# Order of the weighted values and their sums in time attention, and of the first feed-forward products behind band attention

## The chip, the cores and the metric

The kernel runs on one core of a Trainium2 chip. The metric is the device time of one execution in microseconds (us); lower is better. All data is 32-bit floating point. TensorE (PE in the profile) does the matrix products, VectorE (DVE) and GpSimd (POOL) do elementwise work, ScalarE (ACT) evaluates functions, SyncE (SP) issues the transfers.

## The reference, cut to what matters

The input x has 2 batches, 256 times, 128 bands and 128 channels. Three blocks follow one another, each with a layer norm in front and a residual: attention over time (4 heads of 32 channels, causal), attention over the bands (4 heads, a query sees the keys within 16 bands), and a feed-forward of 512 hidden channels with gelu.

```python
def _mha(x, wi, bi, wo, bo, h, mask):
    c = x.shape[-1]; dh = c // h
    q, k, v = jnp.split(x @ wi.T + bi, 3, axis=-1)          # then split into heads
    scores = jnp.einsum('...hqd,...hkd->...hqk', q, k) * (1.0 / np.sqrt(dh)) + mask
    attn = jax.nn.softmax(scores, axis=-1)
    o = jnp.einsum('...hqk,...hkd->...hqd', attn, v)
    o = o.swapaxes(-2, -3).reshape(x.shape)
    return o @ wo.T + bo

xt = _ln(x, ln_t_w, ln_t_b).transpose(0, 2, 1, 3)
x = x + _mha(xt, t_wi, t_bi, t_wo, t_bo, 4, cm).transpose(0, 2, 1, 3)
xf = _ln(x, ln_f_w, ln_f_b)
x = x + _mha(xf, f_wi, f_bi, f_wo, f_bo, 4, bm)
xn = _ln(x, ln_n_w, ln_n_b)
h = jax.nn.gelu(xn @ w1.T + b1, approximate=False)
x = x + (h @ w2.T + b2)
```

## The kernel before

The work is cut into groups of 512 positions: 128 groups of time attention (`OverTime`), then 16 runs, each of 8 groups of band attention (`OverBands`) and the 8 groups of feed-forward (`FeedForward`) on the same data. The groups pass through a software pipeline: iteration n does the scores of group n, the weighted values of group n-1, the output product of group n-2 and the projections of group n+1. Every engine takes its instructions in program order. A product is written to one of eight banks of PSUM, which are handed out in turn.

A product with 128x128 weights can be made as one matmul or as four with 32 weight columns each (128*32 in the profile), which run side by side. `product` does the latter:

```python
def product(path, out, weights, x):
    for c in range(P // D):                       # P = 128, D = 32
        path.tensor.matmul(out[rows_of(c)], weights[:, rows_of(c)], x, start=True, stop=True)
```

It serves `queries_keys` (banks qp, kp), `values` (vp) and `output` (yp) of both attentions. The scores (sp) use 32 rows of the array for each head. The feed-forward uses full matmuls: four products hp for the hidden channels, and sixteen small ones into zp.

In time attention a group has two sequences s of 256 times. The weights p of one sequence and head are three blocks of 128 keys by 128 queries, and a fourth block holds the sum of blocks 1 and 2, so that one matmul with ones makes the softmax denominators (rp) of both query halves. GpSimd adds that block for s = 0 (in `first_mask`), VectorE for s = 1 (`last_sum`, the last step of an iteration):

```python
    def add(self, engine, s):
        engine.tensor_tensor(self.block(s, 3), self.block(s, 1), self.block(s, 2), ALU.add)

    def weigh(self):                                          # OverTime
        path = self.path
        p, v, W = self.p, self.v, self.W
        rp = path.bank([P, 2, 2 * P], "rp")
        sums = p.rearrange("p s h (n q) -> p s h n q", q=P)[:, :, :, 0:4:3, :]
        for h in range(H):
            path.tensor.matmul(rp[rows_of(h), :, :], path.k.ones[:, 0:D], sums[:, :, h], start=True, stop=True)
        op = path.bank([P, 2, 2 * P], "op")
        for s in range(2):
            ...                                               # weighted values of sequence s into op
```

The denominators are inverted on ScalarE, as exp(-ln), and refined on VectorE while the values are divided (the profile calls the tile r0 "r"). The weights of the output product have a minus sign that undoes the sign of oT:

```python
    def invert(self):
        ...
        path.scalar.activation(ln, self.rp, AF.Ln)
        path.scalar.activation(self.r0, ln, AF.Exp, scale=-1.0)

    def divide(self):
        ...
        vector.tensor_tensor(by_rows(t), by_tile(self.rp), by_tile(self.r0), ALU.mult)
        vector.tensor_tensor(by_rows(u), by_tile(self.op), by_tile(self.r0), ALU.mult)
        vector.scalar_tensor_tensor(self.oT, t, 2.0, u, ALU.subtract, ALU.mult)
```

Band attention masks its weights pf outside the band: GpSimd with two selects for each of the first heads (`first_mask`), VectorE with one product for the last `by_vector` heads (`second_mask`); `by_vector` is 1, and 2 in the last group of a run. Its `weigh` makes rp, then op.

The feed-forward makes its four hp in two halves:

```python
    def first_half(self):
        self.hp = {}
        self.hT = ...
        self.hidden((0, 1))          # hp 0 and 1; first_function: their gelus
    def second_half(self):
        self.hidden((2, 3))          # hp 2 and 3; second_function: their gelus
```

The loop of the pipeline; `feeds[2]` says that group n is a feed-forward group, `bands[2]` that it is a band group, index 1 means group n-1; A is 8:

```python
        for n in range(-11, len(groups) + 2):
            feeds = [at(n - 2 + i, FeedForward) for i in range(5)]
            bands = [at(n - 2 + i, OverBands) for i in range(5)]
            do(n + 11, "load")
            do_at(n + 4, OverTime, "statistics")
            if bands[2] and feeds[1]:
                self.scalar.preload_act_table_set(EXP_SET)
            do(n, "first_half", "first_function", "first_mask")
            do_at(n + 2, Attention, "fetch")
            do_at(n + 1, FeedForward, "fetch")
            do_at(n + 2, FeedForward, "normalize", "turn")
            do_at(n + 3, Attention, "normalize", "turn")
            do_at(n + 3, FeedForward, "statistics", "root")
            do_at(n + 4, OverTime, "root")
            if bands[2]:
                do(n, "second_mask")
            do(n - 1, "weigh")
            if not feeds[1]:
                do(n - 1, "invert")
            if bands[2]:
                do(n - 2, "output", "finish")
            do(n - 1, "divide")
            do(n, "second_half", "second_function")
            if not bands[2]:
                do(n, "second_mask", "bias")
                do_at(n + A, OverBands, "bias", "statistics", "root")
            do(n + 1, "queries_keys", "take_query", "take_key")
            if not bands[2]:
                do(n - 2, "output", "finish")
            do(n + 1, "values", "take_values")
            do(n, "last_sum")
```

A group's normalized data xh is turned through memory: VectorE transposes it within 32x32 squares (z), it is written out (turned) and fetched back as xnT an iteration later.

Of the kernel before, what the change touches and what calls it, by code (L numbers as in the profile page):

```python
# [10 lines left out]
F32 = mybir.dt.float32  # L11
# [9 lines left out]
H = 4  # L21
# [414 lines left out]
class Group:  # L436
# [95 lines left out]
    def weigh(self):  # L532
        pass
# [4 lines left out]
    def divide(self):  # L538
        pass
# [8 lines left out]
class Attention(Group):  # L548
# [38 lines left out]
    def invert(self):  # L587
# [4 lines left out]
        self.r0 = path.work.tile([P, NT * P], F32, name="r0", bufs=2)  # L592
        path.scalar.activation(self.r0, ln, AF.Exp, scale=-1.0)

    def divide(self):

        path, vector = self.path, self.path.vector
        t = path.work.tile([P, NT * P], F32, name="t", bufs=2)
        vector.tensor_tensor(by_rows(t), by_tile(self.rp), by_tile(self.r0), ALU.mult)
        u = path.work.tile([P, NT * P], F32, name="u", bufs=2)  # L600
        vector.tensor_tensor(by_rows(u), by_tile(self.op), by_tile(self.r0), ALU.mult)
        self.oT = path.work.tile([P, NT * P], F32, name="oT", bufs=2)
        vector.scalar_tensor_tensor(self.oT, t, 2.0, u, ALU.subtract, ALU.mult)
# [16 lines left out]

def product(path, out, weights, x):

    for c in range(P // D):
        path.tensor.matmul(out[rows_of(c)], weights[:, rows_of(c)], x, start=True, stop=True)


class OverTime(Attention):
# [63 lines left out]
    def last_sum(self):  # L691
        self.add(self.path.vector, 1)

    def weigh(self):
        path = self.path
        p, v, W = self.p, self.v, self.W
        rp = path.bank([P, 2, 2 * P], "rp")
        sums = p.rearrange("p s h (n q) -> p s h n q", q=P)[:, :, :, 0:4:3, :]
        for h in range(H):
            path.tensor.matmul(rp[rows_of(h), :, :], path.k.ones[:, 0:D], sums[:, :, h], start=True, stop=True)  # L700
        op = path.bank([P, 2, 2 * P], "op")
        for s in range(2):
            for h in range(H):
                r = rows_of(h)
                path.tensor.matmul(op[r, s, :], v[:, 2 * s, r], p[:, s, h, 0 : 2 * P], start=True, stop=False)
            for h in range(H):
                r = rows_of(h)
                path.tensor.matmul(
                    op[r, s, P : 2 * P], v[:, 2 * s + 1, r], p[:, s, h, 2 * P : W], start=False, stop=True
                )  # L710
        self.op = op.rearrange("p s q -> p (s q)")
        self.rp = rp.rearrange("p s q -> p (s q)")

# [122 lines left out]
class BoundedPath:  # L836
# [38 lines left out]
    def groups(self, x, out):  # L875
# [29 lines left out]
        for b in range(B):  # L905
            for r0 in range(0, T, RUN):
                run = []
                for t0 in range(r0, r0 + RUN, GB):
                    held = {}


                    def load(g, t0=t0, b=b, held=held):
                        if g == 0:
                            self.quad(held, "x", 4)
                            self.quad(held, "x2", 2 * RUN // GB)
                        for i in range(2 * g, min(2 * g + 2, NT)):
                            nc.sync.dma_start(
                                held["x"][rows_of(i)].rearrange("q g t c -> q (g t) c"),
                                self.of_bands(k.x1[b], t0 + NT * i, NT),
                            )  # L920

                    def store(g, t0=t0, b=b, held=held):
                        for i in range(NT if g % 2 else 0):
                            nc.sync.dma_start(
                                self.of_bands(out[b], t0 + NT * i + g - 1, 2),
                                held["res"][rows_of(i), g - 1 : g + 1].rearrange("q g t c -> q (g t) c"),
                            )

                    def part(name, g, held=held):
                        if name == "res" and name not in held:  # L930
                            self.quad(held, "res", 2)
                        return held[name][:, g]

                    run += [(g, part, load, store) for g in range(NT)]
                for i, (g, part, load, _) in enumerate(run):
                    group = OverBands(self, partial(part, "x", g), partial(part, "x2", g), partial(load, g))
                    if i == len(run) - 1:
                        group.by_vector = 2
                    yield group
                for g, part, _, store in run:  # L940
                    yield FeedForward(self, partial(part, "x2", g), partial(part, "res", g), None, partial(store, g))

    def run(self, x, out):
        groups = list(self.groups(x, out))

        def do(n, *names):
            if 0 <= n < len(groups):
                for name in names:
                    getattr(groups[n], name)()

        def at(n, kind):
            return 0 <= n < len(groups) and isinstance(groups[n], kind)

        def do_at(n, kind, *names):
            if at(n, kind):
                do(n, *names)

        A = RUN // NT

        self.scalar.preload_act_table_set(EXP_SET)  # L960
        for n in range(-11, len(groups) + 2):
            feeds = [at(n - 2 + i, FeedForward) for i in range(5)]
            bands = [at(n - 2 + i, OverBands) for i in range(5)]
            do(n + 11, "load")
            do_at(n + 4, OverTime, "statistics")
            if bands[2] and feeds[1]:
                self.scalar.preload_act_table_set(EXP_SET)
            do(n, "first_half", "first_function", "first_mask")
            do_at(n + 2, Attention, "fetch")
            do_at(n + 1, FeedForward, "fetch")  # L970
            do_at(n + 2, FeedForward, "normalize", "turn")
# [3 lines that stand above are left out]
            if bands[2]:  # L975
                do(n, "second_mask")
            do(n - 1, "weigh")
            if not feeds[1]:
                do(n - 1, "invert")
            if bands[2]:  # L980
                do(n - 2, "output", "finish")
            do(n - 1, "divide")
            do(n, "second_half", "second_function")
            if not bands[2]:
                do(n, "second_mask", "bias")
                do_at(n + A, OverBands, "bias", "statistics", "root")
            do(n + 1, "queries_keys", "take_query", "take_key")
            if not bands[2]:
                do(n - 2, "output", "finish")
            do(n + 1, "values", "take_values")  # L990
            do(n, "last_sum")
# [69 lines left out]
```

## Time and profile before

| What | Value |
|---|---|
| time, median of 3 runs | 2832.48 us (2829.37 to 2876.43) |
| span of the profiled execution | 2826.2 us, 107020 instructions |
| TensorE clock granted | 0.998 of full speed |
| time attention, start of the first rp to that of the last | 54.23 to 1056.75 us, 128 groups |
| a run of 8 band groups and 8 feed-forward groups | about 110 us, 16 of them |
| transfers | 343.90 MB, mean 122 GB/s |

The profile calls a group of instructions by its engine and by the tiles it writes and reads, out<-in: sp, rp, op, qp, kp, vp, yp, hp and zp are the products named above, pt the weights of time attention, pf those of band attention, hT the gelus' output. A row of the timeline gives the start, the duration, the engine, the operation, the tiles, the shapes and how often, with the idle time before it in brackets. Nearly all instructions have one line number, that of a helper, so the tiles tell them apart. Matmuls are pipelined, so the durations of two successive stages overlap; how long a stage holds up the next is read from the distance between two starts. A full-precision product counts as two matmul instructions.

### The profile page before, as it was taken

To read this page: it belongs to the slowest core of one execution; us is meant where nothing else is said; L and a number is where in the kernel's file an instruction comes from. 1 tells how busy PE (TensorE), PEld (TensorE's weight loads), DVE (VectorE), ACT (ScalarE), POOL (GpSimd) and SP (SyncE) were. 2 spreads that over 40 slices of the span, in tenths; PEclk is the share of its full clock that TensorE was granted. 3 is DMA by queue.
4 is the path that set the end of the run, shared out by engine and by line. 5 is a ranking of instruction groups with operands and counts; after the bars stand their busy time and mean duration, and the time that the engine had idled before them with its cause. 6 is when DMAs were issued, how large, how long until landed. Compare 5 with 4: busy or idle time off the path is not lost.

```text
span 2826.2 us, 107020 instructions
## 1 busy us (share of the span) xinstructions
PE 2757.7 (98%) x44070; PEld 1858.9 (66%) x44070; DVE 2264.5 (80%) x6462; ACT 1865.2 (66%) x3408; POOL 2057.9 (73%) x2537
## 2 busy tenths in 40 slices
PE   5999999999999989999999999999999999999998
PEld 3666666666666656766766766666667667667666
DVE  5888888888888898788787787786887877877874
ACT  2777777777777767557557566566575575675664
POOL 3999999999999996676675676676666766656762
PEclk9999999999999999999999999999999999999999
DMA  5455545454554544534434434534435445344333
GB/s 122 126 148 133 140 129 146 131 140 130 147 140 129 135 126 123 144 105 106 128 106 120 129 102 122 131 94 130 115 101 141 106 107 130 102 121 114 87 95 84
DMA packets 471313, 343.90 MB, mean 122 GB/s; under 512 B 43296, under 2 KB 405152, under 8 KB 470816
## 3 DMA queue, kind: packets, MB, share of 16 engines
q1 hardware_dynamic: 469568, 335.92, 45.6%
q8 instruction: 349, 5.72, 0.8%
q14 instruction: 148, 1.21, 0.2%
q10 hardware_dynamic: 1248, 1.05, 0.1%
HBM read 169.03 MB, written 167.77 MB: 119 GB/s over the span
## 4 chain that ended last, share of the span: by engine, by line
PE 93%; DMA 2%; POOL 2%; DVE 2%; issue 0%; SPq 0%; ACT 0%; DVEq 0%; POOLq 0%
PE zp L831 16%; PE hp L831 16%; PE sp L831 13%; PE op L831 9%; PE rp L831 9%; PE qp L831 8%; PE yp L831 7%; PE vp L831 7%; PE kp L831 7%; DMA xnT<-turned 1%; DVE xh L831 1%; POOL pf L831 1%; POOL rstd L831 1%; DMA x<-in_x 1%; POOL pt L831 1%; DMA turned<-z 0%
## 5 line engine op out<-in xcount | busy, mean ns | idle before, releaser
L831 POOL TENSOR_SCALAR_AFFINE_SELECT pf<-pf 128x512 f32<-128x512 f32 x736 | 495.4, 688 | 273.1 <-ACT pf L831 248.0
L831 ACT ACTIVATE hT<-hp,b 128x512 f32<-128x512 f32 x512 | 345.2, 687 | 479.8 <-PE hp L831 470.3
L831 DVE TENSOR_SCALAR xh<-x,mv,rstd 128x128 f32<-128x128 f32 x1536 | 621.7, 465 | 15.4 <-POOL rstd L831 15.4
L831 PEld LDWEIGHTS zp<-w2T_sb,hT 128*128 128x128 f32 x4096 | 476.9, 192 | 56.1 <-issue 51.6
L831 ACT ACTIVATE pt<-sp 128x384 f32<-128x384 f32 x1024 | 419.6, 497 | 104.6 <-PE sp L831 104.6
L831 POOL TENSOR_TENSOR rstd<-rstd,mhalf 128x4 f32<-128x4 f32 x384 | 463.5, 1207 | 32.0
L831 PE MATMUL zp<-w2T_sb,hT 128*128 128x128 f32 x4096 | 480.4, 276 | 0.1
L831 PE MATMUL hp<-xnT,w1f 128*128 128x512 f32 x1024 | 474.8, 599 | 3.3 <-DMA xnT<-turned 3.0
L831 PE MATMUL sp<-qT,kT 32*128 32x128 f32 (+1 forms) x8192 | 398.3, 317 | 0.9 <-ACT kT L831 0.8
L831 POOL TENSOR_SCALAR_AFFINE_SELECT pt<-pt 128x512 f32<-128x512 f32 x512 | 315.3, 636 | 96.6 <-ACT pt L831 96.6
L831 PEld LDWEIGHTS sp<-qT,kT 32*128 32x128 f32 x8192 | 316.5, 186 | 85.8 <-issue 31.8
L831 DVE BATCH_NORM_STATS2 stats<-x 128x6 f32<-128x128 f32 x1536 | 326.8, 273 | 7.8 <-DMA x<-in_x 7.8
L831 POOL TENSOR_SCALAR rstd<-mv 128x4 f32<-128x4 f32 x384 | 94.9, 247 | 318.3 <-DVE mv L831 318.3
L831 ACT ACTIVATE pf<-sp 128x512 f32<-128x512 f32 x512 | 264.4, 603 | 62.5 <-PE sp L831 58.5
L831 PEld LDWEIGHTS hp<-xnT,w1f 128*128 128x128 f32 x1024 | 180.9, 190 | 176.9 <-issue 103.9
L831 PE MATMUL qp<-xnT,wf 128*32 128x512 f32 x2048 | 271.5, 602 | 26.1 <-DMA xnT<-turned 26.1
L831 PEld LDWEIGHTS yp<-wn,oT 128*32 128x32 f32 x8192 | 229.1, 110 | 99.6 <-issue 51.0
L831 DVE STREAM_TRANSPOSE z<-xh 128x512 f32<-128x512 f32 x384 | 273.2, 711 | 18.8 <-DMA turned<-z 5.6
L831 PEld LDWEIGHTS vp<-wf,xnT 128*32 128x32 f32 x8192 | 232.1, 110 | 78.2 <-issue 68.6
L831 DVE TENSOR_TENSOR pf<-pf,band 128x512 f32<-128x512 f32 x144 | 127.1, 892 | 188.8 <-ACT pf L831 181.3
L831 PE MATMUL yp<-wn,oT 128*32 128x128 f32 x8192 | 271.4, 273 | 0.0
L831 PE MATMUL vp<-wf,xnT 128*32 128x128 f32 x8192 | 270.6, 273 | 0.0
(87 smaller groups left out, 4029.4 us busy)
## 6 DMA issues: line engine op xcount, KB each, us to landing
turned<-z SPq DMA_DIRECT2D x1536, 64.0 KB, 2.0
xnT<-turned SPq DMA_DIRECT2D x384, 256.0 KB, 2.7
x<-in_x SPq DMA_DIRECT2D x128, 256.0 KB, 4.7
x<-res SPq DMA_DIRECT2D x256, 128.0 KB, 3.4
x<-x SPq DMA_DIRECT2D x128, 256.0 KB, 4.2
out<-res SPq DMA_DIRECT2D x256, 128.0 KB, 2.8
w1T_sb<-in_w1T ACTq DMA_DIRECT2D x1, 256.0 KB, 3.4
w2T_sb<-in_w2T ACTq DMA_DIRECT2D x1, 256.0 KB, 3.9
```

Of the source, the lines that this page charges most:

```text
L831: return self.tc.keep_in_program_order(emit(*args, **kwargs))
```

## The change

It has four parts.

1. In time attention the weighted values of the first sequence go in front of the denominators, those of the second behind them. They need neither the fourth block nor the second sequence, so that the last addition has time to end.
2. In the first feed-forward group of a run (`turn`) all four hp and their gelus go in front of the last band group's sums and weighted values; the denominators of that band group are inverted on VectorE with its reciprocal, so that the gelus on ScalarE need not make way for ln and exp, and their tables. The output product of the band group before goes in front of the division there. The statistics of one later band group move to the next iteration, and the last band group's mask is shared between the engines like that of the others.
3. Where the group in front is not an attention group, `product` makes one full matmul in place of four of 32 columns, because its neighbours are full matmuls.
4. The banks of PSUM are handed out in the new order: op before rp in time attention, hp, hp before rp and op in the passage.

```diff
--- before.py
+++ after.py
@@ -592,9 +592,20 @@
         self.r0 = path.work.tile([P, NT * P], F32, name="r0", bufs=2)
         path.scalar.activation(self.r0, ln, AF.Exp, scale=-1.0)
 
+    def invert_exactly(self):
+        self.r0 = None
+        self.r = self.path.work.tile([P, NT * P], F32, name="ln", bufs=2)
+        self.path.vector.reciprocal(self.r, self.rp)
+
     def divide(self):
 
         path, vector = self.path, self.path.vector
+        if self.r0 is None:
+            self.oT = path.work.tile([P, NT * P], F32, name="oT", bufs=2)
+            u = path.work.tile([P, NT * P], F32, name="u", bufs=2)
+            vector.tensor_tensor(by_rows(u), by_tile(self.op), by_tile(self.r), ALU.mult)
+            vector.tensor_scalar(self.oT, u, -1.0, None, ALU.mult)
+            return
         t = path.work.tile([P, NT * P], F32, name="t", bufs=2)
         vector.tensor_tensor(by_rows(t), by_tile(self.rp), by_tile(self.r0), ALU.mult)
         u = path.work.tile([P, NT * P], F32, name="u", bufs=2)
@@ -620,6 +631,9 @@
 
 def product(path, out, weights, x):
 
+    if not path.by_columns:
+        path.tensor.matmul(out, weights, x, start=True, stop=True)
+        return
     for c in range(P // D):
         path.tensor.matmul(out[rows_of(c)], weights[:, rows_of(c)], x, start=True, stop=True)
 
@@ -691,23 +705,26 @@
     def last_sum(self):
         self.add(self.path.vector, 1)
 
+    def weigh_one(self, op, s):
+        path, p, v, W = self.path, self.p, self.v, self.W
+        for h in range(H):
+            r = rows_of(h)
+            path.tensor.matmul(op[r, s, :], v[:, 2 * s, r], p[:, s, h, 0 : 2 * P], start=True, stop=False)
+        for h in range(H):
+            r = rows_of(h)
+            path.tensor.matmul(
+                op[r, s, P : 2 * P], v[:, 2 * s + 1, r], p[:, s, h, 2 * P : W], start=False, stop=True
+            )
+
     def weigh(self):
         path = self.path
-        p, v, W = self.p, self.v, self.W
+        op = path.bank([P, 2, 2 * P], "op")
         rp = path.bank([P, 2, 2 * P], "rp")
-        sums = p.rearrange("p s h (n q) -> p s h n q", q=P)[:, :, :, 0:4:3, :]
+        self.weigh_one(op, 0)
+        sums = self.p.rearrange("p s h (n q) -> p s h n q", q=P)[:, :, :, 0:4:3, :]
         for h in range(H):
             path.tensor.matmul(rp[rows_of(h), :, :], path.k.ones[:, 0:D], sums[:, :, h], start=True, stop=True)
-        op = path.bank([P, 2, 2 * P], "op")
-        for s in range(2):
-            for h in range(H):
-                r = rows_of(h)
-                path.tensor.matmul(op[r, s, :], v[:, 2 * s, r], p[:, s, h, 0 : 2 * P], start=True, stop=False)
-            for h in range(H):
-                r = rows_of(h)
-                path.tensor.matmul(
-                    op[r, s, P : 2 * P], v[:, 2 * s + 1, r], p[:, s, h, 2 * P : W], start=False, stop=True
-                )
+        self.weigh_one(op, 1)
         self.op = op.rearrange("p s q -> p (s q)")
         self.rp = rp.rearrange("p s q -> p (s q)")
 
@@ -932,11 +949,8 @@
                         return held[name][:, g]
 
                     run += [(g, part, load, store) for g in range(NT)]
-                for i, (g, part, load, _) in enumerate(run):
-                    group = OverBands(self, partial(part, "x", g), partial(part, "x2", g), partial(load, g))
-                    if i == len(run) - 1:
-                        group.by_vector = 2
-                    yield group
+                for g, part, load, _ in run:
+                    yield OverBands(self, partial(part, "x", g), partial(part, "x2", g), partial(load, g))
                 for g, part, _, store in run:
                     yield FeedForward(self, partial(part, "x2", g), partial(part, "res", g), None, partial(store, g))
 
@@ -961,11 +975,15 @@
         for n in range(-11, len(groups) + 2):
             feeds = [at(n - 2 + i, FeedForward) for i in range(5)]
             bands = [at(n - 2 + i, OverBands) for i in range(5)]
+            turn = feeds[2] and bands[1]
+            self.by_columns = at(n - 1, Attention)
             do(n + 11, "load")
             do_at(n + 4, OverTime, "statistics")
             if bands[2] and feeds[1]:
                 self.scalar.preload_act_table_set(EXP_SET)
             do(n, "first_half", "first_function", "first_mask")
+            if turn:
+                do(n, "second_half", "second_function")
             do_at(n + 2, Attention, "fetch")
             do_at(n + 1, FeedForward, "fetch")
             do_at(n + 2, FeedForward, "normalize", "turn")
@@ -975,17 +993,21 @@
             if bands[2]:
                 do(n, "second_mask")
             do(n - 1, "weigh")
-            if not feeds[1]:
-                do(n - 1, "invert")
-            if bands[2]:
+            do(n - 1, "invert_exactly" if turn else "invert")
+            if bands[2] or turn:
                 do(n - 2, "output", "finish")
             do(n - 1, "divide")
-            do(n, "second_half", "second_function")
+            if not turn:
+                do(n, "second_half", "second_function")
             if not bands[2]:
                 do(n, "second_mask", "bias")
-                do_at(n + A, OverBands, "bias", "statistics", "root")
+                do_at(n + A, OverBands, "bias")
+                if at(n - 1, FeedForward) and at(n - 2, OverBands):
+                    do_at(n + A - 1, OverBands, "statistics", "root")
+                if not turn:
+                    do_at(n + A, OverBands, "statistics", "root")
             do(n + 1, "queries_keys", "take_query", "take_key")
-            if not bands[2]:
+            if not bands[2] and not turn:
                 do(n - 2, "output", "finish")
             do(n + 1, "values", "take_values")
             do(n, "last_sum")
```

## The prediction

> **What bounds the kernel now.** I read the page first (busy shares, then the chain that ended last), then the timeline of TensorE in one stretch of time attention and in one passage from band attention to the feed-forward, and last the other engines in the same two stretches. The page says that TensorE is the bound and that almost nothing else stands on the chain:
>
> ```profile
> PE 2757.7 (98%) x44070; PEld 1858.9 (66%) x44070; DVE 2264.5 (80%) x6462; ACT 1865.2 (66%) x3408; POOL 2057.9 (73%) x2537
> PE 93%; DMA 2%; POOL 2%; DVE 2%; issue 0%; SPq 0%; ACT 0%; DVEq 0%; POOLq 0%
> ```
>
> So a change can gain only where TensorE takes longer over a stage than the stage has to, and that is read from the distance between the starts of stages, not from the busy share. In time attention (columns: start, duration in us, engine, ...):
>
> ```profile
> 600.14 1.06 PE L831 MATMUL vp<-wf,xnT 128*32 128x128 f32 x32
> 601.13 0.94 PE L831 MATMUL sp<-qT,kT 32*128 32x256 f32 x16
> 602.18 1.06 PE L831 MATMUL rp<-pt,ones 128*32 128x512 f32 x8
> 603.04 1.51 PE L831 MATMUL op<-pt,v 128*32 128x256 f32 x32
> 604.48 0.94 PE L831 MATMUL sp<-qT,kT 32*128 32x256 f32 x16
> 605.35 1.07 PE L831 MATMUL qp<-xnT,wf 128*32 128x512 f32 x8
> ...
> 601.00 1.04 DVE L831 TENSOR_TENSOR pt<-pt 128x512 f32<-128x512 f32 x1
> ```
>
> The reader should see two equal sets of scores, sp: the second gives way to qp after 605.35 - 604.48 = 0.87 us, the first to the sums rp only after 602.18 - 601.13 = 1.05. The sums read the block that DVE's last addition writes (pt<-pt, 601.00 to 602.04), and start 0.14 after it. They wait 1.05 - 0.87 = 0.18 us for it, and the same is found in the next iterations (608.95 and 610.00, 616.76 and 617.82). The iteration repeats every 7.82 us (the starts of rp).
>
> The passage to the feed-forward:
>
> ```profile
> 1545.00 1.06 PE L831 MATMUL yp<-wn,oT 128*32 128x128 f32 x32
> 1546.02 1.96 PE L831 MATMUL hp<-xnT,w1f 128*128 128x512 f32 x4
> 1547.90 1.46 PE L831 MATMUL rp<-pf,ones 128*32 128x512 f32 x8
> 1548.79 1.45 PE L831 MATMUL op<-pf,v 128*32 128x128 f32 x32
> 1550.17 1.98 PE L831 MATMUL hp<-xnT,w1f 128*128 128x512 f32 x4
> 1552.08 1.08 PE L831 MATMUL yp<-wn,oT 128*32 128x128 f32 x32
> 1553.09 1.98 PE L831 MATMUL hp<-xnT,w1f 128*128 128x512 f32 x4
> 1554.91 3.75 PE L831 MATMUL zp<-w2T_sb,hT 128*128 128x128 f32 x32
> ...
> 1547.00 1.27 DVE L831 TENSOR_TENSOR pf<-pf,band 128x512 f32<-128x512 f32 x2
> ```
>
> Products in column tiles (128*32) and full ones (128*128) alternate. Undisturbed, eight full hp take 3.44 us (1566.72 to 1570.15), so four take 1.72; here they take 1.88, 1.91, 1.82. A yp between other column products takes 0.87; in front of hp it takes 1.01 to 1.02. The op at 1548.79 takes 1.38 instead of 0.87.
>
> **What the Trainium skill says.** "TensorEngine Tiling (Array Packing)", section Key Properties: changing the tiling mode, not just the tile, drains TensorE. The trace agrees: from column tiles to full 0.14 on yp and 0.10 on the next hp, 0.24 in all; from full to column tiles 0.09 on hp and about 0.01 on what follows, 0.10. "Trainium Kernel Development and Optimization", section Performance Expectations, calls matmul busy time a bad metric because matmuls are pipelined; here both the wait of 0.18 and the drains lie inside the 98%. "ScalarE: Activation LUTs", section What ACT_TABLE_LOAD costs: 1283 ns for a table load, as in the trace (80 loads, mean 1283). "VectorE: DVE Perf Modes", section First, the fixed hardware budget: a reciprocal is an iterative divide with a repeat count of 8. The kernel has no large reciprocal, so no row here shows its cost. My estimate from that page: 8 cycles an element at its 0.96 GHz, 512 x 8 / 0.96 = 4.3 us; if the repeat is pipelined, 0.66 like the other DVE reads of a bank (t<-rp,r, 665 ns).
>
> **The change, part by part.**
>
> Time attention. op of the first half goes in front of rp, op of the second half behind. Nothing is added; the number of tile switches is the same. sp now gives way to op after 0.87, as it does to qp. The first op takes half of the 1.28 us that its 768 columns need at the rate of rp (0.86 for 512), 0.64. rp could then start at 601.13 + 0.87 + 0.64 = 602.64, and its operand is there at 602.04 + 0.14 = 602.18: the wait is gone with 0.46 to spare. Gain 0.18 per iteration. Of the 127 distances between iterations 119 are the steady 7.8 (the first is 8.51); in the last 7, at 8.3 to 9.7 us, DVE hardly pauses because it also makes the statistics of the first bands, and there I count nothing. 119 x 0.18 = 21.4 us.
>
> First feed-forward group behind the bands (16 times). The order was yp | hp hp | rp op | hp hp | yp | hp hp | zp | hp hp | yp | hp. It becomes yp | hp hp hp hp | rp op yp | hp hp zp hp hp, and the last yp as full products. Switches into full products fall from 4 to 2, out of them from 3 to 1: 2 x 0.24 + 2 x 0.10 = 0.68 us. The full yp has the form of zp, 3.57 / 4 = 0.89, against 0.87: -0.02. The stall in op: of its 1.38, 0.14 are the switch, the remaining 0.37 come from DVE's mask of two heads, which ends at 1548.27 while rp started at 1547.90. With four hp in front, rp starts at 1546.02 + 1.88 + 1.72 = 1549.6, when the one head left on DVE is long done (about 1547.6), and POOL's six selects instead of four (1543.89 + 6 x 0.68) end near 1548.0. So +0.37. Together 1.03, times 16 = 16.5 us.
>
> Start of the next bands (15 times). The projections of the first two groups become full. hp into qp and zp into qp lose their switch: 0.09 + 0.02 and 0.10 + 0.02 (zp takes 3.77 there, 3.57 elsewhere, half of the surplus being its start after sp). 0.23 x 15 = 3.5 us.
>
> Off the path. Three table loads (1.28 each) and the pair ln and exp (0.63 each) leave ScalarE in each passage, 5.1 us, but TensorE did not wait there: zp starts without a gap. On DVE t (0.66) and the fused oT (0.69) leave, the reciprocal and a plain multiply (about 0.4) come, one band mask (0.64) leaves, and statistics of one group (1.1) move one iteration later. POOL gains two selects, 1.4 us.
>
> Sum: 21.4 + 16.5 + 3.5 = 41.4; 2832.5 - 41.4 = 2791 us.
>
> **The rivals.** First, another wait takes the place of the 0.18. The banks of op and rp trade places in the ring of eight, so yp now takes the bank that DVE's u frees (at 606.5) instead of t's (605.9). yp would start near 606.9 and needs its weights about 0.2 before, so some 0.2 to 0.4 are left; if yp did wait 0.1, time attention would lose 12 of its 21. POOL pauses 0.67 and DVE 1.0 per iteration, so a period of 7.64 fits both, which speaks against a new bound; but POOL is 90% busy there, and if its longer instructions shift against DVE's, half of the gain could go. Result about 2803.
>
> Second, the reciprocal is dear. With 4.3 us on DVE, the last oT would be ready near 1558.8 and its yp comes near 1559.5; just in time. DVE would run about 2.5 us late into the second and third feed-forward group, whose inputs pass through memory twice (2.0 and 2.7 us to landing); I count about 2 us of room there. If that is used up, 0.5 to 1 us is lost 16 times. Six of the 16 passages already wait up to 0.9 us for xnT at the first hp, so this path is tight. Result about 2800 to 2805. For it: the estimate of 8 cycles. Against: DVE has idle stretches of 0.9 to 3.5 us from the fourth group on.
>
> Third, a larger gain: relieved of waits, the last seven iterations of time attention shorten too (1.9 us above the steady period in the worst), and the 0.48 us lost in the last sp (1541.66 to 1543.24 against 1.10) go with the DVE's load. The first is bound by DVE without pauses and the second lies ahead of what is changed, so I give it little; result about 2775.
>
> **Range and chances.** All three terms are read from waits that recur to 0.01 us, so the direction is fairly sure; the sizes depend on the wait not coming back. Predicted 2791 us, range 2777 to 2808. Faster by over 2% would need 56.7 us, more than all the terms together: 0.06. Slower by over 2% would need a stall that nothing in the profile shows: 0.01. Within 2%: 0.93.
>
> **What would show it.** Right: the iteration of time attention at 7.64 us with sp to op at 0.87; in the passage four hp at 3.6, op at 0.87, hp to qp without surplus; 32 table loads instead of 80. Wrong: rp still starting 0.14 behind DVE's addition, a pause ahead of yp (bank ring) or of hp with xnT as the releaser (late DVE), a reciprocal whose duration shows up as later oT. The prediction would be wrong above all if the 7.82 stayed and merely another stage of the iteration grew.

## The result and the profile after

| | median | range | ratio to before, 95% interval |
|---|---|---|---|
| before | 2830.93 us | 2828.15 to 2876.43 | |
| changed | 2793.24 us | 2791.73 to 2793.65 | 0.9868 [0.9851, 0.9885] |

The changed kernel is 1.3% faster: 37.7 us between the medians. One execution of the kernel before took 2876.43 us; without it the median before is 2829.37 us and the gain 36.1 us, and all ratios and all medians below leave such executions out. The profiled spans differ by 2826.2 - 2791.8 = 34.4 us. The page of the changed kernel, busy shares and the chain that ended last:

```profile
PE 2733.2 (98%) x42534; PEld 1844.4 (66%) x42534; DVE 2302.8 (82%) x6446; ACT 1800.7 (65%) x3328; POOL 2062.7 (74%) x2569
PE 89%; DVE 4%; DMA 3%; POOL 3%; SPq 1%; issue 1%; ACT 0%; DVEq 0%; POOLq 0%
```

TensorE is still busy 98%, so the page alone doesn't show where the gain came from. The chain says a little more: TensorE's share fell from 93 to 89%, and DVE, transfers, GpSimd and the transfer queue took its place. Something else now ends last more often.

An iteration of time attention in the timeline of the changed kernel (start, duration, engine, ...):

```profile
604.05 0.94 PE L848 MATMUL sp<-qT,kT 32*128 32x256 f32 x16
604.92 0.86 PE L848 MATMUL op<-pt,v 128*32 128x256 f32 x16
605.60 1.04 PE L848 MATMUL rp<-pt,ones 128*32 128x512 f32 x8
...
604.12 1.10 DVE L848 TENSOR_TENSOR pt<-pt 128x512 f32<-128x512 f32 x1
...
603.46 1.22 POOL L848 TENSOR_SCALAR_AFFINE_SELECT pt<-pt 128x512 f32<-128x512 f32 x2
```

The first scores now give way after 604.92 - 604.05 = 0.87 us instead of 1.05. DVE's addition ends at 605.22, and rp starts at 605.60, so the sums no longer wait for it. The distance between the starts of rp is 7.63 us, from 7.82.

The passage to the feed-forward:

```profile
1520.23 3.70 PE L848 MATMUL hp<-xnT,w1f 128*128 128x512 f32 x8
1523.86 1.07 PE L848 MATMUL rp<-pf,ones 128*32 128x512 f32 x8
1524.74 1.06 PE L848 MATMUL op<-pf,v 128*32 128x128 f32 x32
1525.62 1.06 PE L848 MATMUL yp<-wn,oT 128*32 128x128 f32 x32
1526.61 1.98 PE L848 MATMUL hp<-xnT,w1f 128*128 128x512 f32 x4
1528.43 3.73 PE L848 MATMUL zp<-w2T_sb,hT 128*128 128x128 f32 x32
1532.00 1.88 PE L848 MATMUL hp<-xnT,w1f 128*128 128x512 f32 x4
1533.72 1.05 PE L848 MATMUL yp<-wn,oT 128*128 128x128 f32 x8
1534.61 1.88 PE L848 MATMUL hp<-xnT,w1f 128*128 128x512 f32 x4
1536.33 3.73 PE L848 MATMUL zp<-w2T_sb,hT 128*128 128x128 f32 x32
...
1527.33 3.33 DVE L848 RECIPROCAL ln<-rp 128x512 f32<-128x512 f32 x1
```

The stretch behind the first zp in the kernel before:

```profile
1558.50 1.88 PE L831 MATMUL hp<-xnT,w1f 128*128 128x512 f32 x4
1560.31 1.08 PE L831 MATMUL yp<-wn,oT 128*32 128x128 f32 x32
1561.32 1.99 PE L831 MATMUL hp<-xnT,w1f 128*128 128x512 f32 x4
1563.14 3.73 PE L831 MATMUL zp<-w2T_sb,hT 128*128 128x128 f32 x32
```

From start to start, four hp take 3.63 us, op takes 0.88 where it took 1.38, and the hp, yp and hp behind the first zp take 1.72, 0.89 and 1.72 where they took 1.81, 1.01 and 1.82. The reciprocal, whose cost no row of before could show, takes 3.3 us.

Both traces cut at the same marks show where the 34 us are. The marks are the starts of the stages named; a run is 8 band groups and the 8 feed-forward groups behind them, and the values (us) are means over all runs.

| Stretch | before | changed | times | sum |
|---|---|---|---|---|
| first rp to last rp of time attention | 1002.52 | 980.01 | 1 | -22.5 us |
| first hp to first zp | 8.74 | 8.29 | 16 | -7.2 |
| first zp to second zp | 8.25 | 7.90 | 16 | -5.6 |
| second zp to seventh zp | 35.04 | 35.29 | 16 | +4.0 |
| seventh zp to eighth zp | 9.21 | 9.09 | 15 | -1.8 |
| eighth zp to the next run's first hp | 48.82 | 48.67 | 15 | -2.4 |

The fourth row is a loss that the prediction had only as a rival. Before, the five groups between the second and the seventh zp took 35.03 or 35.04 in every run; now they take 35.03 to 36.75. The surplus lies in the hp in front of the seventh zp: 1571.74 - 1567.92 = 3.82 us in the run shown above (its lines stand under "The fetch ahead in the queue"), where the kernel before took 3.44.

### The profile page after: what moved, and what is told of

Same layout as the page of the kernel before. It is cut to its first block, busy times and chain, and to the rows that moved or that the text cites. A ratio compares the mean times of both kernels' runs of the same rounds, so it can differ in the third digit from the quotient of the medians.

```text
span 2791.8 us, 103916 instructions
## 1 busy us (share of the span) xinstructions
PE 2733.2 (98%) x42534; PEld 1844.4 (66%) x42534; DVE 2302.8 (82%) x6446; ACT 1800.7 (65%) x3328; POOL 2062.7 (74%) x2569
## 3 DMA queue, kind: packets, MB, share of 16 engines
q14 instruction: 148, 1.21, 0.1%
q10 hardware_dynamic: 1248, 1.05, 0.1%
## 4 chain that ended last, share of the span: by engine, by line
PE 89%; DVE 4%; DMA 3%; POOL 3%; SPq 1%; issue 1%; ACT 0%; DVEq 0%; POOLq 0%
PE zp L848 16%; PE hp L848 15%; PE sp L848 12%; PE op L848 9%; PE qp L848 8%; PE rp L848 7%; PE vp L848 7%; PE kp L848 7%; PE yp L848 7%; DMA xnT<-turned 1%; DVE xh L848 1%; POOL pf L848 1%; DMA turned<-z 1%; POOL rstd L848 1%; POOL pt L848 1%
## 5 line engine op out<-in xcount | busy, mean ns | idle before, releaser
L848 POOL TENSOR_SCALAR_AFFINE_SELECT pf<-pf 128x512 f32<-128x512 f32 x768 | 520.9, 694 | 270.6 <-ACT pf L848 244.3
L848 POOL TENSOR_TENSOR rstd<-rstd,mhalf 128x4 f32<-128x4 f32 x384 | 446.9, 1164 | 32.0
L848 POOL TENSOR_SCALAR_AFFINE_SELECT pt<-pt 128x512 f32<-128x512 f32 x512 | 323.0, 652 | 79.6 <-ACT pt L848 79.6
L848 POOL TENSOR_SCALAR rstd<-mv 128x4 f32<-128x4 f32 x384 | 88.6, 231 | 298.7 <-DVE mv L848 297.5
L848 PE MATMUL qp<-xnT,wf 128*32 128x512 f32 (+1 forms) x1856 | 270.6, 600 | 26.1 <-DMA xnT<-turned 26.1
L848 PEld LDWEIGHTS yp<-wn,oT 128*32 128x32 f32 (+1 forms) x7808 | 234.1, 111 | 83.8 <-issue 61.8
L848 PEld LDWEIGHTS vp<-wf,xnT 128*32 128x32 f32 (+1 forms) x7424 | 237.3, 113 | 75.0 <-issue 65.5
L848 PE MATMUL vp<-wf,xnT 128*32 128x128 f32 (+1 forms) x7424 | 271.9, 273 | 0.5 <-DVE t L848 0.5
L848 PE MATMUL yp<-wn,oT 128*32 128x128 f32 (+1 forms) x7808 | 271.1, 273 | 0.3 <-DVE t L848 0.3
L848 DVE TENSOR_TENSOR pf<-pf,band 128x512 f32<-128x512 f32 x128 | 117.4, 917 | 184.8 <-ACT pf L848 177.3
```

The lines of the kernel that those rows point to most:

```text
L848: return self.tc.keep_in_program_order(emit(*args, **kwargs))
```

## The experiments

**The order in time attention alone.** The kernel before with the new order of op and rp:

```diff
-        rp = path.bank([P, 2, 2 * P], "rp")
+        op = path.bank([P, 2, 2 * P], "op")
+        rp = path.bank([P, 2, 2 * P], "rp")
+        self.weigh_one(op, 0)                   # op of one sequence
         ...                                     # rp
-        op = path.bank([P, 2, 2 * P], "op")
-        for s in range(2): ...                  # op of both sequences
+        self.weigh_one(op, 1)
```

> The kernel before with the new order in time attention alone (op of the first sequence, rp, op of the second). Theory (the only gain there is rp's wait for the last addition, and it does not come back): the period of time attention 7.63 us as in the changed kernel, 119 x 0.19 = 22 us less, about 2809 us; 110.0 us per run of bands and feed-forward as before. Rival (the time attention gained through the full products at its start or through what follows, and not through this order): above 2820 us, period above 7.7.

Measured: 2807.49 us (2806.61 to 2809.25), beside 2830.1 for the kernel before; ratio 0.992 [0.9903, 0.9938]. The period is 7.63 us. The 22.6 us are what the theory gave; the rival is out.

**The sums without the last addition.** What the order did is not yet why it did it: op behind sp might cost TensorE less than rp behind sp. Here the order of before stays, and rp's operand is another block. The denominators of the later queries then leave out a part of their sum; DVE still makes the addition.

```diff
-        sums = p.rearrange("p s h (n q) -> p s h n q", q=P)[:, :, :, 0:4:3, :]
+        sums = p.rearrange("p s h (n q) -> p s h n q", q=P)[:, :, :, 0:3:2, :]
```

> The kernel before, rp in front of op, but rp reads the third block of weights in place of the fourth, so that it no longer reads what DVE's last addition writes (the denominators of the later queries then leave out part of their sum; the addition itself is still made). Theory (rp waited for that addition and for nothing else): the first sp gives way to rp after 0.87 us as to op in the changed kernel, period 7.63, about 2808 as with the new order alone. Rival (the order itself is cheaper for TensorE, op behind sp instead of rp): the period stays at 7.82, about 2830.

Measured: 2808.21 us, ratio 0.9926 [0.9903, 0.9948], period 7.63. The timeline of this kernel:

```profile
603.33 0.94 PE L831 MATMUL sp<-qT,kT 32*128 32x256 f32 x16
604.19 1.06 PE L831 MATMUL rp<-pt,ones 128*32 128x512 f32 x8
...
603.20 1.03 DVE L831 TENSOR_TENSOR pt<-pt 128x512 f32<-128x512 f32 x1
```

rp follows sp after 0.86 us, and starts at 604.19 although the addition ends at 604.23. The wait was for that addition and for nothing else; the order of the matmuls as such brings nothing measurable (2808.2 us here, 2807.5 with the new order).

**The addition earlier.** If rp waits for the addition, an earlier addition should help too. In the kernel before, DVE's last addition moves in front of its addition of the output product:

```diff
             if not bands[2]:
-                do(n - 2, "output", "finish")
-            do(n + 1, "values", "take_values")
-            do(n, "last_sum")
+                do(n - 2, "output")
+            do(n, "last_sum")
+            if not bands[2]:
+                do(n - 2, "finish")
+            do(n + 1, "values", "take_values")
```

> The kernel before with its order of rp and op in time attention; DVE's last addition goes in front of its addition of the output product instead of behind. Theory (rp waits for that addition alone): the addition can start when GpSimd's first select ends, at 600.9 on the scale of the trace of before instead of 601.0 by about 0.1 us; rp follows 0.14 behind its end, the period falls from 7.82 to between 7.70 and 7.74, 119 x 0.08 to 0.12 = 10 to 14 us less, about 2818. Rival (op behind sp costs TensorE less than rp behind sp, whatever DVE does): the period stays 7.82 and the time near 2830.

Measured: 2941.71 us (2940.01 to 2942.29), ratio 1.04 [1.0385, 1.0416]: neither of the two. The period is 8.78 us. Its timeline:

```profile
602.87 1.08 PE L831 MATMUL yp<-wn,oT 128*32 128x128 f32 x32 [0.51 <-DVE t L831]
604.75 0.94 PE L831 MATMUL sp<-qT,kT 32*128 32x256 f32 x16
606.04 1.06 PE L831 MATMUL rp<-pt,ones 128*32 128x512 f32 x8 [0.36 <-DVE pt L831]
...
604.14 1.76 DVE L831 TENSOR_TENSOR pt<-pt 128x512 f32<-128x512 f32 x1
...
603.64 1.71 POOL L831 TENSOR_TENSOR res<-x,orow 128x512 f32<-128x512 f32 x1
```

The addition takes 1.76 us, because it now starts while GpSimd adds the bias, until 605.35. It ends at 605.90, 0.55 after that. The same holds in the kernel before: the row of GpSimd there is

```profile
600.27 1.22 POOL L831 TENSOR_SCALAR_AFFINE_SELECT pt<-pt 128x512 f32<-128x512 f32 x2
```

which ends at 601.49, and the addition ends at 602.04, again 0.55 later; in the changed kernel 604.68 and 605.22, 0.54. "SBUF — State Buffer" of the Trainium skill, section SBUF: two separate sides, says that DVE and GpSimd share a port pair as an exclusive lock, and that a DVE instruction with two inputs from SBUF waits for a GpSimd instruction that reads SBUF and holds it. The three pairs fit that, and they are not picked: in each of these three traces all 128 additions end 0.54 to 0.56 us after the GpSimd instruction that was under way when they started, while their own durations go from 0.65 to 1.76. On this reading the addition did not need 1.04 us of DVE's time; it waited for GpSimd and then ran for about 0.55, and starting it earlier only put it against a longer GpSimd instruction. The normalization behind it grew as well (xh 2.78 us in place of 1.54), DVE no longer pauses between one t (602.16) and the next (610.94), and its work between the two takes the whole 8.78 us: it is the bound. That the whole of the surplus comes from this lock is not shown; what is shown is that DVE's rows grow and its pauses go.

**Column tiles everywhere.** The changed kernel without its full products in attention:

```diff
-            self.by_columns = at(n - 1, Attention)
+            self.by_columns = True
```

> The changed kernel with products in column tiles everywhere. Theory (a change between column tiles and full products costs TensorE 0.24 us on the way into full ones and 0.10 out of them): the yp between hp and hp costs 0.34 - 0.02 us more 16 times, the projections of two groups 0.23 us more 15 times: 5.1 + 3.5 = 8.6 us more than the changed kernel, about 2802. Rival (the passage gained by the new order and the tables alone, the width of the products does not matter): within 2 us of the changed kernel, 2793.

Measured: 2802.6 us (2801.7 to 2803.6), ratio 0.9901 [0.9884, 0.9919]; 9.4 us more than the changed kernel. The passage there:

```profile
1534.12 1.88 PE L848 MATMUL hp<-xnT,w1f 128*128 128x512 f32 x4
1535.93 1.08 PE L848 MATMUL yp<-wn,oT 128*32 128x128 f32 x32
1536.94 1.98 PE L848 MATMUL hp<-xnT,w1f 128*128 128x512 f32 x4
1538.76 3.73 PE L848 MATMUL zp<-w2T_sb,hT 128*128 128x128 f32 x32
```

From start to start 1.81, 1.01 and 1.82 us, in place of 1.72, 0.89 and 1.72: 0.31 more. First to second zp takes 8.22 instead of 7.90 in all 16 runs, 5.1 us; the other end of a run, where the next bands begin, gives 0.12 + 0.16 us (the last two rows of the table above), 15 times, 4.2. The switches are paid for as read from the trace of before.

**The reciprocal away, and twice.** Two opposite edits of the changed kernel. First, ln and exp on ScalarE as before, but behind the gelus:

```diff
-            do(n - 1, "invert_exactly" if turn else "invert")
+            if turn:
+                self.scalar.preload_act_table_set(EXP_SET)
+            do(n - 1, "invert")
```

> The changed kernel with ln and exp on ScalarE instead of the reciprocal in the passage, behind the four gelus, with one load of their table set in front and one of the gelu's behind. Theory (the reciprocal of 3.3 us keeps DVE late until the last feed-forward group, whose xnT then arrives late; TensorE never waits for ScalarE's tables): the stretch from the second to the seventh zp returns from a mean of 35.29 us to 35.03, 4 us less in all, about 2789. Rival (the table loads in the passage were what cost time): 2 x 1.28 us of loads and 1.26 of functions come back into the passage, up to 16 x 1 us or more, 2800 to 2820.

Second, the reciprocal a second time, with the same result:

```diff
         self.path.vector.reciprocal(self.r, self.rp)
+        self.path.vector.reciprocal(self.r, self.rp)
```

> The changed kernel with the reciprocal in the passage made twice, nothing else. Theory (DVE's lateness reaches the last feed-forward group): 3.3 us more of lateness, of which DVE's pauses up to there take up little; the wait at that group's first hp grows in every run by 2 to 3.3 us, 16 x 2 to 16 x 3.3 = 32 to 53 us more, about 2825 to 2846. Rival (the wait there has another cause, transfers of other groups on the way): the stretch from the second to the seventh zp stays near 35.3, the time within 5 us of 2793.

Measured: on ScalarE 2789.88 us (2789.62 to 2791.19), ratio 0.9856 [0.9838, 0.9873]; second to seventh zp 35.03 or 35.04 in 15 of 16 runs, mean 35.09. The two table loads and two functions came back on ScalarE, and TensorE lost nothing. Twice: 2844.9 us (2842.12 to 2845.45), ratio 1.0051 [1.0033, 1.0069], slower than before the change. TensorE's groups in that kernel (count, then busy us and mean ns, then idle us and what ended it):

```profile
L849 PE MATMUL hp<-xnT,w1f 128*128 128x512 f32 x1024 | 476.3, 598 | 29.1 <-DMA xnT<-turned 20.5 <-DVE xh L849 7.3 <-ACT r L849 0.8
L849 PE MATMUL yp<-wn,oT 128*32 128x128 f32 (+1 forms) x7808 | 272.2, 273 | 18.5 <-DVE oT L849 17.4 <-ACT hT L849 0.8 <-DVE t L849 0.3
```

The second reciprocal costs 51.7 us between the medians, 48.6 between the profiled spans. Of these, 46 lie in two places: hp waits for late inputs (second to seventh zp 36.78, 1.49 more, 24 us in 16 runs), as the theory had it, and the last yp waits for oT (first to second zp 9.28, 1.38 more, 22 us), which the expectation had left out. One DVE instruction of 3.3 us in the passage is nearly free, a second one costs 51.7 / 16 = 3.2 us each time.

**The fetch ahead in the queue.** Why does the lateness show only in the last group of a run? In the changed kernel:

```profile
1558.68 0.71 DVE L848 STREAM_TRANSPOSE z<-xh 128x512 f32<-128x512 f32 x1
1559.32 3.11 DVE L848 TENSOR_SCALAR xh<-x,mv,rstd 128x128 f32<-128x128 f32 x4
1562.47 0.71 DVE L848 STREAM_TRANSPOSE z<-xh 128x512 f32<-128x512 f32 x1
...
1559.42 5.55 SPq L489 DMA_DIRECT2D turned<-z  x8
1566.45 0.84 SPq L494 DMA_DIRECT2D xnT<-turned  x2
...
1567.92 3.98 PE L848 MATMUL hp<-xnT,w1f 128*128 128x512 f32 x8
1571.74 3.73 PE L848 MATMUL zp<-w2T_sb,hT 128*128 128x128 f32 x32
```

The last feed-forward group's z is there at 1559.39. But in the one queue of transfers stand eight writes, four of them of the next band group, whose z comes 3.8 us later (1563.18); the fetch of the feed-forward group is issued behind them, together with the band group's own, at 1566.45; such a fetch takes 2.7 us to land (the median of all). The edit puts that fetch ahead of the band group's writes:

```diff
+        self.fetched = False                     # ahead of the loop
...
-            do_at(n + 1, FeedForward, "fetch")
+            if not self.fetched:
+                do_at(n + 1, FeedForward, "fetch")
             do_at(n + 2, FeedForward, "normalize", "turn")
+            self.fetched = at(n + 2, FeedForward) and at(n + 3, Attention)
+            if self.fetched:
+                do(n + 2, "fetch")
```

> The changed kernel; only the fetch of the last feed-forward group of a run goes into the queue of transfers ahead of the writes of the band group behind it. Theory (DVE's lateness of some us hurts only because that fetch stands in the queue behind writes that wait for the band group's z, which comes 3 us after the feed-forward group's): the wait at the last group's first hp goes although the reciprocal stays, the stretch from the second to the seventh zp falls from 35.29 to about 35.03, 4 us less, about 2789. Rival (the feed-forward group's own z is too late, or the transfers are slow for another reason): the stretch stays near 35.3 and the time near 2793.

Measured: 2789.03 us (2786.99 to 2790.33), ratio 0.986 [0.9845, 0.9875]; second to seventh zp on the mean 35.04, with the reciprocal in place. The same place in that kernel:

```profile
1558.03 4.56 SPq L489 DMA_DIRECT2D turned<-z  x6
1562.82 0.34 SPq L494 DMA_DIRECT2D xnT<-turned  x1
1563.21 0.90 SPq L489 DMA_DIRECT2D turned<-z  x2
...
1566.50 3.60 PE L848 MATMUL hp<-xnT,w1f 128*128 128x512 f32 x8
1569.94 3.73 PE L848 MATMUL zp<-w2T_sb,hT 128*128 128x128 f32 x32
```

The fetch is issued at 1562.82, 3.7 us ahead of the start of that stage of hp instead of 1.5, and the stage takes 3.44. (In the trace it stands ahead of the last two of the band group's writes, not of all four, and ahead of that group's fetch.) In that trace the loss was made by the two together: a DVE that is late, and a fetch that queues behind a write that waits for it.

A late DVE is not the only thing that makes this stage wait, though. The kernel with the new order of time attention alone has no reciprocal, and still 2 of its 16 runs took 36.80 and 35.84 us from the second to the seventh zp. In the first of them:

```profile
1458.09 0.84 SPq L494 DMA_DIRECT2D xnT<-turned  x2
...
1460.97 1.88 PE L834 MATMUL hp<-xnT,w1f 128*128 128x512 f32 x4
1464.37 1.96 PE L834 MATMUL hp<-xnT,w1f 128*128 128x512 f32 x4 [1.52 <-DMA xnT<-turned]
```

The fetch was issued 2.9 us ahead of that stage, as in the kernel before, but was slow to land. In the changed kernel 2 of 16 runs (36.75 and 35.88) make 2.6 of the 4 us and eight others, 0.05 to 0.40 us each, the rest. So the reciprocal takes away room, and how much of the 4 us is its own is not settled by one trace; the early fetch gives the room back in either case.

**Both.** The two edits in one kernel:

> The changed kernel with ln and exp on ScalarE in the passage and the early fetch, both edits. Theory (both take away the same wait): 2788 to 2790, not below the better of the two by more than 1 us; zp to zp 35.03 in every run. Rival (two separate losses): 2785 to 2786.

Measured: 2789.46 us (2788.24 to 2790.69), ratio 0.9865 [0.985, 0.9879]; 35.03 or 35.04 in every run. They take away the same wait, not two. The ratios' intervals of the changed kernel and of these three overlap. Their times, 2786.99 to 2791.19, lie below those of the changed kernel, 2791.73 to 2793.65; but the kernel before, run beside each, differed by as much as 1.3 us itself (2828.9 to 2830.1). What is shown is the stretch: 35.09, 35.04 and 35.03 in place of 35.29, 16 times, 3 to 4 us.

**One head on VectorE.** The kernel before with `group.by_vector = 1` in the last group of a run:

> The kernel before with DVE masking one head instead of two in the last band group of a run, GpSimd the other three. Theory (the op of that group was held back up to 0.4 us by DVE's two masks, in 10 or 11 of 16 passages): from the first hp to the first zp 8.50 us in all passages instead of 8.74 on the mean, 16 x 0.24 = 3.9 us less, about 2826.5. Rival (GpSimd's two more selects come as late as DVE's second mask did): the same 8.7 or more, time 2830 or above.

Measured: 2828.62 us beside 2828.86, ratio 1.0002 [0.9993, 1.0012]: nothing, as the rival had it. The profile read here is that of another execution of the same kernel:

> The same as the kernel with one head on VectorE, for another profile. The time did not fall. If GpSimd's selects are the new end of the mask, op or rp behind the first hp start after GpSimd's sixth select in the passages that take 8.8 us, and the first hp to the first zp is again 8.5 in some passages and 8.8 in others. If DVE's mask was never the cause, the stretch has the same values and GpSimd ends well ahead.

The time of that execution is 2831.05 us. First hp to first zp is 8.75 us on the mean, 8.50 to 8.55 in some passages and 8.80 to 8.83 in most others, as expected. A passage of that profile:

```profile
1659.81 1.36 PE L831 MATMUL rp<-pf,ones 128*32 128x512 f32 x8
1660.69 1.35 PE L831 MATMUL op<-pf,v 128*32 128x128 f32 x32
1661.98 1.98 PE L831 MATMUL hp<-xnT,w1f 128*128 128x512 f32 x4
...
1655.80 4.27 POOL L831 TENSOR_SCALAR_AFFINE_SELECT pf<-pf 128x512 f32<-128x512 f32 x6 [1.16 <-ACT pf L831]
```

GpSimd's sixth select ends at 1660.07, behind the start of rp at 1659.81, and op still takes 1.29 us. The mask's end moved from DVE to GpSimd and stayed where it was. Sharing the mask does not take the stall out of op by itself. In the changed kernel, where two more hp stand in front, rp starts at 1523.86, a microsecond behind GpSimd's sixth select (1518.40 + 4.44 = 1522.84), and op takes 0.88. The two hp with the mask of before were not run.

**The division first in band attention.** The last sp of a run takes 1.58 us from start to start, in the kernel before and in the changed one, against 1.10 in the others. In the kernel with both edits, DVE's division now goes in front of its addition of the output product:

```diff
             if bands[2] or turn:
-                do(n - 2, "output", "finish")
+                do(n - 2, "output")
             do(n - 1, "divide")
+            if bands[2] or turn:
+                do(n - 2, "finish")
```

> The changed kernel with ln and exp on ScalarE, the early fetch, and in band attention DVE's division in front of its addition of the output product instead of behind. Theory (the last sp of a run takes 1.58 us instead of 1.10 because two of its banks come free with DVE's t and u, which are late by the statistics of the first feed-forward groups; t and u now come 0.6 us earlier): that sp falls to about 1.10, 16 x 0.48 = 7.7 us less, about 2782. Rival (the banks are free in time and sp waits for something else): it stays at 1.58, about 2789.

Measured: 2793.56 us, ratio 0.9871 [0.9848, 0.9893]; that sp takes mostly 1.65 to 1.67. The expectation failed, and so did its rival: that sp got longer. In this kernel:

```profile
1625.47 0.31 PEld L848 LDWEIGHTS sp<-qT,kT 32*128 32x128 f32 x6 [0.20 <-ACT kT L848]
1626.04 0.96 PEld L848 LDWEIGHTS sp<-qT,kT 32*128 32x128 f32 x26 [0.27 <-DVE u L848]
...
1624.71 0.68 DVE L848 TENSOR_TENSOR t<-rp,r 128x512 f32<-128x512 f32 x1
1625.31 0.68 DVE L848 TENSOR_TENSOR u<-op,r 128x512 f32<-128x512 f32 x1
```

The loads stop after the third head and go on at 1626.04, when u ends (1625.99). In the kernel before they went on when t ended (1542.10, loads at 1542.16), with DVE's order x, t, u there and t, u, x here. Each time it is the second of the three that frees the bank of the fourth head: it looks as if banks are handed out in the order in which they come free, so that putting u before x gave that head u's bank. That sp waits for a bank which DVE frees late fits both traces; how to free it earlier was not found, and the order of handing out is argued from these two traces only.

## Why the prediction was right

**Time attention.** Predicted 7.64 us and 21.4 us in all; measured 7.63 and 22.5. The step "the wait is gone with 0.46 to spare" held with 605.60 - 605.22 = 0.38 to spare. The order alone brought 22.6 us, and taking away only what rp waited for brought 21.3. The last seven iterations stayed at 8.3 to 9.7, as counted; DVE is busy 98% of them, but GpSimd 99%, so that the prediction's reason, DVE alone, is not shown.

**The passage.** Predicted 1.03 us a passage, measured 0.45 + 0.35 = 0.80. The switches were sized right: 0.32 was predicted for the stretch behind the first zp, 0.35 was found there, and column tiles put back cost 0.32. The term that was mis-sized is the stall in op, 0.37. It was read from one passage and multiplied by 16; over all 16 passages of before, op takes 1.21 us on the mean and 0.99 where it isn't held, so 0.22: 0.15 too much. Where hp had waited for xnT, rp came later and the mask was in time. And the explanation of it was half right: DVE's second mask did end last, but the head given to GpSimd ends no earlier. A further 0.1 us a passage went to waits for xnT: the stretch takes 8.16 to 8.22 us in 12 passages, but 8.41 to 9.08 in the other four.

**The next bands.** Predicted 0.23, measured 0.12 + 0.16 = 0.28. The 0.16 is a difference of means that waits for xnT spread; the shortest such stretches, 48.56 before and 48.44 now, differ by 0.12, which gives 0.24.

**The reciprocal.** "VectorE: DVE Perf Modes", section First, the fixed hardware budget, has a repeat count of 8, from which the estimate of 4.3 us came; the 16 reciprocals take 3324 ns on the mean, 512 elements at 6.2 cycles of 0.96 GHz, and the measurement decides. The second rival had the mechanism, late inputs through memory, and looked for it in the second and third group; it came in the last one, where two groups' transfers share the queue, and cost at most 4 us and not 8 to 16. That oT would be just in time was right: in the passage shown oT was ready at 1532.25 and yp started at 1533.72, 1.5 us later, which a second reciprocal used up.

**The other rivals.** The first (yp waiting for u's bank) did not appear: kp gives way to yp after 0.86 us as before. That such a wait is possible is seen where the addition was moved: with DVE late, yp waited 0.51 us for t. The third (gains beyond the terms) did not appear.

**The tables.** 32 loads instead of 80, and nothing gained by it: with the early fetch in both, the kernel with 2 loads a passage put back takes 2789.46 us, the one without them 2789.03.

**The sum.** The table gives -22.5 - 12.8 + 4.0 - 4.2 = -35.5 us, of which the start of the kernel took back 0.8. The prediction, -41.4, was 5.9 us too far: 4.0 for the late group and 3.7 for the passage, less 1.1 and 0.7 by which time attention and the next bands gained more than predicted. That 2791 comes so near to 2793.24 is partly luck: the 41.4 us were taken from 2832.5; taken from 2829.4 they give 2788. The mechanism, waits and switches inside the 98%, was right in each of the three terms.

## What to carry to other kernels

Where the bound engine is busy 98%, compare the distance between stage starts of equal stages: a wait of 0.18 us that recurs 119 times, and switches of 0.1 to 0.24 us, lie inside the busy time and can be added up. Multiply a stall only after looking at all its occurrences. When work is moved to an engine off the path, follow its lateness through queues that keep order: the reciprocal was free where it stood, and the wait came 40 us later; moving one fetch removed it.

## What the runs showed of the hardware that was not expected

A DVE addition of two 128x512 blocks ended 0.54 to 0.56 us after the end of the GpSimd instruction it met, whatever that was, in all 128 iterations of three kernels; in the iterations shown the addition was 1.04, 1.10 and 1.76 us long. Moving that one instruction ahead of another of 0.69 us changed a period of 7.82 us to 8.78.

The switch of the products' form seems to cost differently in the two directions. Around the yp between full products (the rows with column tiles everywhere) the hp in front takes 1.81 instead of 1.72, so about 0.1 us from full to column tiles; yp takes 1.01 instead of the 0.87 between column products, and the hp behind it 1.82 instead of 1.72, so about 0.24 from column tiles to full. The run shows the sum of the two, 0.32 us with the 0.02 by which the full yp is slower; the division is read from the distances alone.
